# Two cross-attention layers on one core: first weights in parts, key-bias products moved, last batch projected with queries on partitions, a norm in two operations

## The chip, the cores and the metric

The kernel runs on one core of one Trainium2 chip. The metric is the time of one execution on the device, in microseconds. The kernel before took 739.87 us as the median of three runs (737.16 to 740.08). Its profiled execution took 736.62 us, of which the span from the first to the last instruction is 734.8 us.

## The reference, cut to what matters

Two layers of cross attention read the same context. There are 8 batches of 100 queries of width 1024, and 1444 context rows of width 512 per batch. All values are 32-bit floats.

```python
# layer 0: softmax over the 1444 keys, an output projection, a residual
Q = query @ Wq + bq;  K = key @ Wk + bk;  V = key @ Wv + bv
weights = softmax((Q @ K.T) / 32, axis=keys)
x = query + (weights @ V) @ Wo + bo

# layer 1: softmax over the 100 queries, a residual, a norm over the width of 1024
q = x @ Wq + bq;  k = latent @ Wk + bk;  v = latent @ Wv + bv
w = softmax((q @ k.T) / 32, axis=queries)
x = w @ v + x
return (x - mean(x)) * rsqrt(var(x) + 1e-6) * gamma + beta
```

The kernel never forms K and V. It multiplies weights with weights first (Wq Wk^T, and Wv Wo in layer 0), so that attention works on the context rows of width 512. Three consequences matter here. A bias of the keys gives one number per query, the sum over x and a vector Wq bk; the kernel calls it c0 in layer 0 and c1 in layer 1. In layer 1 the weights of a query don't sum to one, because the softmax runs over queries, so bv is multiplied by the sum of a query's weights (`r`). And in layer 1 the weighted context rows (`A1`, width 512) are multiplied by Wv (`wv1`) at the end.

## The kernel before: the parts that the change and its steps touch

The program order of TensorE is the order of the source. The orders of the other engines are decided when the program is built. Every matmul on 32-bit floats runs as two passes, so that a line with 64 products of the source shows 128 instructions.

```python
    psum = ctx.enter_context(tc.tile_pool(name="psum", bufs=8, ...))     # 8 banks
    ident = const.tile([P, P], ...);  make_identity(nc, ident)
    ones = const.tile([P, P], ...);   nc.vector.memset(ones, 1.0)

    def column(name, layout):              # six small bias columns
        nc.scalar.dma_start(out=t, in_=a[name].rearrange(layout, c=EC))

    def weight_products(name, left, right, l_width, r_width, scaled):
        for h in range(EC):                                     # 8 blocks of 128 rows
            st = unit(f"{name}_{h}")
            nc.sync.dma_start(out=st[:, :l_width], in_=lsrc[:, h, :])
            nc.sync.dma_start(out=st[:, l_width:], in_=rsrc[:, h, :])
            for ps, (i, j) in zip(banks, blocks):               # 8 products of 128x512
                nc.tensor.matmul(ps, st[:, i*P:(i+1)*P], st[:, l_width + j*512 : ...], ...)   # L111
            ...                                                 # VectorE: columns scaled and summed
```

The start of the program, with the key-bias products of layer 0 between the queries and the next weights:

```python
    wqk0, (acc_c, acc_u) = weight_products("qk0", ...)
    ...                                                         # xT loaded, u0, bqbk0, wqbk0
    for g in range(B // G):
        gT[0][g] = queries(0, g, wqk0, u0)                      # L175
    for g in range(B // G):                                     # two groups of four batches
        acc = key_bias_sums(f"kb0_{g}", g * GT, (g + 1) * GT, wqbk0)   # VectorE, L163/L165, one buffer "kb"
        for i in range(G):
            nc.tensor.matmul(ps[:T, b:b+1], acc[:, i*T:(i+1)*T], ones[:, 0:1], ...)   # L203
    nc.vector.tensor_scalar(c0, ps[:T, :B], SCALE, bqbk0[:T], ALU.mult, ALU.add)      # L204
    wvo, (acc_o,) = weight_products("vo0", ...)
    nc.vector.tensor_tensor(out_bias, out_bias, totals("bvo_ps", acc_o, EC), ALU.add) # L137, L208
    wqk1, (acc_c, acc_u) = weight_products("qk1", ...)
```

The end of the program, layer 1 from its weighted rows on:

```python
    def attend1(s, dst):
        ...                                # VectorE: part and wsum, the weights of a query summed
        weighted_rows(b, w, c, dst, ...)   # L256, then a VectorE copy from PSUM to dst (L264)
        nc.tensor.matmul(ps[:T, 0:1], wsum[:n], ones[:n, 0:1], ...)        # L382
        nc.vector.tensor_copy(s["r"], ps[:T, 0:1])

    def project1(b0, n, A):                # embedding on partitions, n*T queries as columns
        for e in range(EC):
            for k in range(LC):
                nc.tensor.matmul(ps[:, :n*T], wv1[:, k, e*P:(e+1)*P], A[:, k, :n*T], ...)   # L392
            nc.vector.tensor_tensor(to, to, ps[:, :n*T], ALU.add)                           # L396, to = xT[:, e, t0:t1]

    def finish(s):
        for j in range(2):
            for e in range(4):
                nc.tensor.transpose(ps[:T, ...], xT[:, 4*j+e, b*T:(b+1)*T], ident)          # L406
            nc.vector.scalar_tensor_tensor(z[:, half], bv1[:T, half], s["r"], ps[:T, :], ALU.mult, ALU.add)  # L408
            nc.vector.bn_stats(stats[:, j, :], z[:, half])                                  # L409
        nc.vector.bn_aggr(mv, ...)                                                          # L411
        nc.vector.tensor_scalar(rstd, mv[:, 1:2], EPS, None, ALU.add)                       # L413
        nc.gpsimd.tensor_tensor(rstd, rstd, mhalf[:T], ALU.pow)                             # L414
        nc.vector.tensor_scalar(z, z, mv[:, 0:1], rstd, ALU.subtract, ALU.mult)             # L415
        nc.gpsimd.tensor_tensor(z, z, gamma[:T], ALU.mult)                                  # L416
        nc.gpsimd.tensor_tensor(z, z, beta[:T], ALU.add)                                    # L417
        nc.gpsimd.dma_start(out=out[b], in_=z)                                              # L418

    for b in range(B):
        if b % 2 == 0:
            A1 = work.tile([P, LC, GT], ...)
        attend1(batches[b], A1[:, :, b % 2 * T : (b % 2 + 1) * T])
        if b == 0:
            ...                                            # queries and c1 of the second group
        if b + 2 < B:
            scores1(batches[b + 2], c1[(b + 2) // G])      # L343
        if b % 2:
            project1(b - 1, 2, A1)
            finish(batches[b - 1])
            finish(batches[b])
```

Of the kernel before, what the change touches and what calls it, by code (L numbers as in the profile page):

```python
# [30 lines left out]
P = 128  # L31
# [9 lines left out]
G = 4  # L41
# [6 lines left out]
def two_layer_cross_attention(ctx: ExitStack, tc: tile.TileContext, a: dict, out: bass.AP):  # L48
# [20 lines left out]
        return work.tile([P, S], F32, tag="prob", name=name, bufs=3)  # L69


    ident = const.tile([P, P], F32, tag="ident", name="ident")
    make_identity(nc, ident)
    ones = const.tile([P, P], F32, tag="ones", name="ones")
    nc.vector.memset(ones, 1.0)
    mhalf = const.tile([P, 1], F32, tag="mhalf", name="mhalf")
    nc.vector.memset(mhalf, -0.5)

    def column(name, layout):
        t = const.tile([P, EC], F32, tag=name, name=name)  # L80
        nc.scalar.dma_start(out=t, in_=a[name].rearrange(layout, c=EC))
        return t

    cols = {
# [6 lines left out]
    def weight_products(name, left, right, l_width, r_width, scaled):  # L91

        accs = []
        for v, side in scaled:
            if (l_width if side == 0 else r_width) == E:
                accs.append(row(f"{name}_{v}"))
            else:  # L100
                accs.append(work.tile([P, L], F32, tag="half", name=f"{name}_{v}", bufs=1))
        blocks = [(i, j) for i in range(l_width // P) for j in range(r_width // 512)]
        banks = [bank(f"{name}_{i}_{j}") for i, j in blocks]
        lsrc = a[left].rearrange("(p c) n -> p c n", c=EC)
        rsrc = a[right].rearrange("(p c) n -> p c n", c=EC)
        for h in range(EC):
            st = unit(f"{name}_{h}")
            nc.sync.dma_start(out=st[:, :l_width], in_=lsrc[:, h, :])
            nc.sync.dma_start(out=st[:, l_width:], in_=rsrc[:, h, :])
            for ps, (i, j) in zip(banks, blocks):  # L110
                nc.tensor.matmul(  # L111
                    ps,
                    st[:, i * P : (i + 1) * P],
                    st[:, l_width + j * 512 : l_width + (j + 1) * 512],
                    start=(h == 0),
                    stop=(h == EC - 1),
                )
            for acc, (v, side) in zip(accs, scaled):
                src = st[:, :l_width] if side == 0 else st[:, l_width:]
                if h == 0:  # L120
                    nc.vector.tensor_scalar(acc, src, cols[v][:, h : h + 1], None, ALU.mult)
                else:
                    nc.vector.scalar_tensor_tensor(acc, src, cols[v][:, h : h + 1], acc, ALU.mult, ALU.add)  # L123
        dst = weights.tile([P, l_width // P, r_width], F32, tag="w", name=name)
        for n, (ps, (i, j)) in enumerate(zip(banks, blocks)):
            to = dst[:, i, j * 512 : (j + 1) * 512]
            if n % 2:
                nc.scalar.copy(to, ps)
            else:
                nc.vector.tensor_copy(to, ps)  # L130
        return dst, accs
# [24 lines left out]

    def key_bias_sums(name, t0, t1, wqbk):

        acc = work.tile([P, GT], F32, tag="kb", name=name)
        for k in range(EC):  # L160
            src = xT[:, k, t0:t1]
            if k == 0:
                nc.vector.tensor_scalar(acc, src, wqbk[:, k : k + 1], None, ALU.mult)  # L163
            else:
                nc.vector.scalar_tensor_tensor(acc, src, wqbk[:, k : k + 1], acc, ALU.mult, ALU.add)  # L165
        return acc
# [27 lines left out]
    gT = [[None, None], [None, None]]  # L194
    for g in range(B // G):
        gT[0][g] = queries(0, g, wqk0, u0)
    c0 = const.tile([T, B], F32, tag="c0", name="c0")
    ps = bank("c0_ps")
    for g in range(B // G):
        acc = key_bias_sums(f"kb0_{g}", g * GT, (g + 1) * GT, wqbk0)  # L200
        for i in range(G):
            b = g * G + i
            nc.tensor.matmul(ps[:T, b : b + 1], acc[:, i * T : (i + 1) * T], ones[:, 0:1], start=True, stop=True)  # L203
    nc.vector.tensor_scalar(c0, ps[:T, :B], SCALE, bqbk0[:T], ALU.mult, ALU.add)  # L204


    wvo, (acc_o,) = weight_products("vo0", "L0_xattn_WvT", "L0_xattn_Wo", L, E, (("L0_xattn_bv", 1),))
    nc.vector.tensor_tensor(out_bias, out_bias, totals("bvo_ps", acc_o, EC), ALU.add)  # L208


    wqk1, (acc_c, acc_u) = weight_products(
# [38 lines left out]
    def weighted_rows(b, w, c, dst, name):  # L250

        ps = bank(name)
        for m in range(MC):
            r = held(m)
            for k in range(LC):
                nc.tensor.matmul(  # L256
                    ps[:, k * T : (k + 1) * T],
                    c[m // CQ][:r, m % CQ, k * P : (k + 1) * P],
                    w[:r, m, :],
                    start=(m == 0 and k == 0),  # L260
                    stop=(m == MC - 1),
                    skip_group_check=True,
                )
        nc.vector.tensor_copy(dst, ps[:, :GT].rearrange("p (c t) -> p c t", t=T))  # L264


    def scores0(s):
# [50 lines left out]
    def key_bias1(g):  # L318

        acc = key_bias_sums(f"kb1_{g}", g * GT, (g + 1) * GT, wqbk1)  # L320
        ps = bank(f"c1_ps{g}")
        nc.tensor.matmul(ps[:, :GT], ones, acc, start=True, stop=True)
        c1 = work.tile([P, GT], F32, tag="c1", name=f"c1_{g}", bufs=2)
        nc.vector.tensor_scalar(c1, ps[:, :GT], SCALE, bqbk1, ALU.mult, ALU.add)
        return c1

# [40 lines left out]
            )  # L367
        s["w"] = w

    def attend1(s, dst):  # L370
        b, w = s["b"], s["w"]
        c = load_rows(b)
        part = work.tile([P, GT], F32, tag="kb", name=f"part_{b}")[:, :T]
        wsum = work.tile([P, T], F32, tag="wsum", name=f"wsum_{b}", bufs=1)
        last = MC - 1
        nc.vector.tensor_copy(wsum[: held(last)], w[: held(last), last, :])
        nc.vector.tensor_reduce(part[:MR], w[:MR, :last, :].rearrange("p c t -> p t c"), AX.X, ALU.add)
        nc.vector.tensor_tensor(wsum[:MR], wsum[:MR], part[:MR], ALU.add)
        weighted_rows(b, w, c, dst, f"A1_{b}")
        ps = bank(f"wsum_ps_{b}")  # L380
        n = held(last)
        nc.tensor.matmul(ps[:T, 0:1], wsum[:n], ones[:n, 0:1], start=True, stop=True)  # L382
        s["r"] = small.tile([T, 1], F32, tag="r", name=f"r_{b}", bufs=3)
        nc.vector.tensor_copy(s["r"], ps[:T, 0:1])

    def project1(b0, n, A):

# [7 lines left out]
            to = xT[:, e, t0:t1]  # L395
            nc.vector.tensor_tensor(to, to, ps[:, : n * T], ALU.add)  # L396

    def finish(s):

        b = s["b"]  # L400
        z = row(f"z_{b}")[:T]
        stats = small.tile([T, 2, 6], F32, tag="stats", name=f"stats_{b}")
        for j in range(2):
            ps = bank(f"z_{b}_{j}")
            for e in range(4):
                nc.tensor.transpose(ps[:T, e * P : (e + 1) * P], xT[:, 4 * j + e, b * T : (b + 1) * T], ident)  # L406
            half = slice(j * 512, (j + 1) * 512)
            nc.vector.scalar_tensor_tensor(z[:, half], bv1[:T, half], s["r"], ps[:T, :], ALU.mult, ALU.add)  # L408
            nc.vector.bn_stats(stats[:, j, :], z[:, half])  # L409
        mv = small.tile([T, 2], F32, tag="mv", name=f"mv_{b}")  # L410
        nc.vector.bn_aggr(mv, stats.rearrange("p a n -> p (a n)"))  # L411
        rstd = small.tile([T, 1], F32, tag="rstd", name=f"rstd_{b}")
        nc.vector.tensor_scalar(rstd, mv[:, 1:2], EPS, None, ALU.add)  # L413
        nc.gpsimd.tensor_tensor(rstd, rstd, mhalf[:T], ALU.pow)  # L414
        nc.vector.tensor_scalar(z, z, mv[:, 0:1], rstd, ALU.subtract, ALU.mult)  # L415
        nc.gpsimd.tensor_tensor(z, z, gamma[:T], ALU.mult)  # L416
        nc.gpsimd.tensor_tensor(z, z, beta[:T], ALU.add)  # L417
        nc.gpsimd.dma_start(out=out[b], in_=z)  # L418


    batches = [{"b": b} for b in range(B)]
# [26 lines left out]

    scores1(batches[0], c1[0])
    weighted0(G + 3)  # L450
    bv1 = row_on_all("L1_xattn_bv")
    gamma = row_on_all("L1_xattn_gamma")
    beta = row_on_all("L1_xattn_beta")
# [1 line left out]
    project0(1, A0[1])  # L455
    wv1 = weights.tile([P, LC, E], F32, tag="w", name="wv1")
    nc.gpsimd.dma_start(out=wv1, in_=a["L1_xattn_Wv"].rearrange("(c p) e -> p c e", p=P))
    A1 = None
    for b in range(B):
        if b % 2 == 0:  # L460
            A1 = work.tile([P, LC, GT], F32, tag="AT", name=f"A1T_{b}", bufs=2)
        attend1(batches[b], A1[:, :, b % 2 * T : (b % 2 + 1) * T])
        if b == 0:
            gT[1][1] = queries(1, 1, wqk1, u1)
            c1[1] = key_bias1(1)
        if b + 2 < B:
            scores1(batches[b + 2], c1[(b + 2) // G])
        if b % 2:
            project1(b - 1, 2, A1)
            finish(batches[b - 1])  # L470
            finish(batches[b])


# [22 lines left out]
```

## Time and profile before

| what | value |
|---|---|
| time, median of 3 | 739.87 us |
| span of the profiled execution | 734.8 us |
| TensorE busy | 702.8 us, 96% |
| VectorE busy | 251.5 us, 34% |
| ScalarE busy | 78.0 us, 11% |
| GpSimd busy | 49.5 us, 7% |
| mean granted TensorE clock | 0.981 |
| moved by DMA | 124.73 MB, 170 GB/s over the span |

PE is TensorE's matmul, PEld its weight load, DVE VectorE, ACT ScalarE, POOL GpSimd, SP SyncE. A line number such as L203 is a line of the kernel. In the chain of work that ended last and in the timeline the first column is the start in us from the start of the span, the second the duration in us, and "x96" the number of instructions merged. In the list of waits the three numbers are the total in us, how many there were, and the longest in us. In a table by stretches of time the columns are the stretch, its length, the busy time of each engine with its instructions in brackets, the granted clock as a share of full speed, the share of the DMA engines, and GB/s.

### The profile page before, as it was taken

Reading aid. Unit: us, or ns where it says so; the run is one execution under the profiler, and the core shown is the slowest. Engines: PE = TensorE matmul, PEld = TensorE weight load, DVE = VectorE, ACT = ScalarE, POOL = GpSimd, SP = SyncE. Lnnn points to the kernel's source line nnn. Section 1 sums busy time; section 2 is a strip of 40 time slices with the busy share of each in tenths; the row PEclk is TensorE's granted clock in tenths of the full one; section 3 lists DMA queues with packets and bytes.
Section 4 is the critical chain, followed back from the end, with each engine's and each line's share of the span. In section 5 each row is a group of like instructions: output and inputs, shape, how many; then the busy total and the mean of one; then the engine's idle time right before and its main releaser. Section 6 shows DMA issues by size and latency. Waiting matters only on the chain.

```text
span 734.8 us, 8978 instructions
## 1 busy us (share of the span) xinstructions
PE 702.8 (96%) x3848; PEld 514.7 (70%) x3848; DVE 251.5 (34%) x404; ACT 78.0 (11%) x261; POOL 49.5 (7%) x42
## 2 busy tenths in 40 slices
PE   6999997999999999999999999999999999999980
PEld 3445553444445678885675889867799999999980
DVE  6346002321002412224300224440245745745633
ACT  0001010001001201110000113200112012012000
POOL 0000000000000000000000000000000600600606
PEclk9999998999999999999999999999999999999995
DMA  8952001333344999999052999958197798794101
GB/s 302 389 217 86 1 0 41 92 123 88 116 117 92 281 279 263 248 264 276 7 162 71 249 258 270 262 123 266 44 245 198 218 257 221 215 244 113 46 0 45
DMA packets 70696, 124.73 MB, mean 170 GB/s; under 512 B 4897, under 2 KB 39713, under 8 KB 70657
## 3 DMA queue, kind: packets, MB, share of 16 engines
q1 hardware_dynamic: 66912, 117.19, 57.9%
q0 software_dynamic: 1984, 6.95, 3.0%
q8 instruction: 30, 0.49, 0.3%
q10 hardware_dynamic: 1760, 0.02, 0.1%
q14 instruction: 10, 0.07, 0.0%
HBM read 120.87 MB, written 3.28 MB: 169 GB/s over the span
## 4 chain that ended last, share of the span: by engine, by line
PE 83%; issue 9%; POOL 4%; DVE 2%; DMA 1%; POOLq 0%; SPq 0%
PE A L256 18%; PE qk L111 15%; PE g L175 12%; PE s L278 11%; PE s L343 8%; PE vo L111 8%; PE o L311 6%; PE o L392 3%; POOL z L416 2%; POOL z L417 1%; PE pT L301 1%; DVE z L415 1%; DVE kb L165 1%; DMA qk<-in_L_xattn_WkT 1%; PE wqbk_ps L137 1%
## 5 line engine op out<-in xcount | busy, mean ns | idle before, releaser
L256 PE MATMUL A<-w,c 120*128 120x100 f32 (+1 forms) x1536 | 174.7, 275 | 0.0
L256 PEld LDWEIGHTS A<-w,c 120*128 120x128 f32 (+1 forms) x1536 | 172.8, 192 | 1.0
L111 PE MATMUL qk<-qk 128*128 128x512 f32 x256 | 112.7, 603 | 5.6 <-DMA qk<-in_L_xattn_WkT 5.6
L111 PEld LDWEIGHTS qk<-qk 128*128 128x128 f32 x256 | 49.4, 194 | 67.3 <-issue 61.5
L175 PE MATMUL g<-xT,qk 128*128 128x400 f32 x256 | 86.7, 500 | 0.0
L343 PE MATMUL s<-g1T,cT 128*120 128x100 f32 (+1 forms) x768 | 83.1, 270 | 0.0
L343 PEld LDWEIGHTS s<-g1T,cT 128*120 128x120 f32 (+1 forms) x768 | 82.2, 186 | 0.3 <-issue 0.2
L278 PE MATMUL s<-cT,g0T 128*100 128x360 f32 (+1 forms) x256 | 80.3, 473 | 0.0
L175 PEld LDWEIGHTS g<-xT,qk 128*128 128x128 f32 x256 | 48.4, 190 | 36.5
L278 PEld LDWEIGHTS s<-cT,g0T 128*100 128x100 f32 x256 | 43.0, 170 | 34.1 <-issue 1.7
L111 PE MATMUL vo<-vo 128*128 128x512 f32 x128 | 56.8, 607 | 0.0
L361 ACT ACTIVATE w<-w,negmax 120x100 f32<-120x100 f32 (+1 forms) x96 | 35.1, 367 | 147.4 <-DVE negmax L359 147.4
L111 PEld LDWEIGHTS vo<-vo 128*128 128x128 f32 x128 | 24.9, 196 | 31.2 <-issue 31.2
L281 DVE TENSOR_SCALAR p<-s,c 100x360 f32<-100x360 f32 (+1 forms) x32 | 19.0, 594 | 78.6 <-PE s L278 78.5
L392 PE MATMUL o<-A1T,wv 128*128 128x200 f32 x256 | 44.1, 333 | 0.6 <-DVE A1T L264 0.6
L392 PEld LDWEIGHTS o<-A1T,wv 128*128 128x128 f32 x256 | 43.2, 190 | 0.7 <-DVE A1T L264 0.7
L311 PE MATMUL o<-A0T,vo 128*128 128x400 f32 x128 | 43.3, 499 | 0.0
L311 PEld LDWEIGHTS o<-A0T,vo 128*128 128x128 f32 x128 | 24.2, 190 | 18.3
L123 DVE SCALAR_TENSOR_TENSOR qk_L_xattn_bk<-qk,L_xattn_bk,qk_L_xattn_bk 128x1024 f32<-128x1024 f32 x14 | 18.0, 1284 | 33.6 <-DMA qk<-in_L_xattn_WqT 33.6
L446 POOL DMA_DIRECT2D L_xattn_bv<-in_L_xattn_bv x1 | 0.7, 696 | 405.5 <-PE pT L301 405.5
L130 DVE COPY qk<-qk 128x512 f32<-128x512 f32 x8 | 5.5, 691 | 56.3 <-PE qk L111 56.3
L264 DVE COPY A0T<-A 128x400 f32<-128x400 f32 x8 | 4.6, 574 | 57.0 <-PE A L256 57.0
(77 smaller groups left out, 385.5 us busy)
## 6 DMA issues: line engine op xcount, KB each, us to landing
cT<-in_ctxT SPq DMA_DIRECT2D x64, 728.0 KB
c<-in_ctx SPq DMA_DIRECT2D x64, 720.0 KB
qk<-in_L_xattn_WqT SPq DMA_DIRECT2D x16, 512.0 KB
qk<-in_L_xattn_WkT SPq DMA_DIRECT2D x16, 256.0 KB
vo<-in_L_xattn_Wo SPq DMA_DIRECT2D x8, 512.0 KB
xT<-in_xT SPq DMA_DIRECT2D x2, 1600.0 KB
out<-z POOLq DMA_DIRECT2D x8, 400.0 KB, 3.7
vo<-in_L_xattn_WvT SPq DMA_DIRECT2D x8, 256.0 KB
```

The costliest lines, as they stand in the source:

```text
L111: nc.tensor.matmul(ps, st[:, i * P : (i + 1) * P], st[:, l_width + j * 512 : l_width + (j + 1) * 512], start=(h == 0), stop=(h == EC - 1),)
L123: nc.vector.scalar_tensor_tensor(acc, src, cols[v][:, h : h + 1], acc, ALU.mult, ALU.add)
L137: nc.tensor.matmul(ps[:, c : c + 1], acc[:, c * P : (c + 1) * P], ones[:, 0:1], start=True, stop=True)
L175: nc.tensor.matmul(ps[:, :GT], w[:, k, c * P : (c + 1) * P], xT[:, k, t0:t1], start=(k == 0), stop=(k == EC - 1))
L256: nc.tensor.matmul(ps[:, k * T : (k + 1) * T], c[m // CQ][:r, m % CQ, k * P : (k + 1) * P], w[:r, m, :], start=(m == 0 and k == 0), stop=( ...
L278: nc.tensor.matmul(ps[:T, :n], q0[:, k, t0 : t0 + T], cT[q][:, k, :n], start=(k == 0), stop=(k == LC - 1))
L281: nc.vector.tensor_scalar(p[:, q * QR : q * QR + n], ps[:T, :n], SCALE, c0[:, b : b + 1], ALU.mult, ALU.add)
L311: nc.tensor.matmul(ps[:, :GT], wvo[:, k, e * P : (e + 1) * P], A[:, k, :], start=(k == 0), stop=(k == LC - 1))
L343: nc.tensor.matmul(ps[:r, (m - m0) * T : (m - m0 + 1) * T], cT[m // CQ][:, k, o : o + r], q1[:, k, t0 : t0 + T], start=(k == 0), stop=(k = ...
L361: nc.scalar.activation(w[:r, m, :], w[:r, m, :], AF.Exp, bias=negmax[:r, m : m + 1], accum_out=total[:r, m : m + 1])
L392: nc.tensor.matmul(ps[:, : n * T], wv1[:, k, e * P : (e + 1) * P], A[:, k, : n * T], start=(k == 0), stop=(k == LC - 1))
L416: nc.gpsimd.tensor_tensor(z, z, gamma[:T], ALU.mult)
```

## The change

It does these things.

- Eight products of `ones` with `ones` stand at the head of TensorE's program, ahead of any data. `ones` is made first.
- The first block of weights comes in three transfers instead of two: the right operand and half of the left one from SyncE, the other half of the left one from ScalarE. The six bias columns are loaded from GpSimd's queue.
- The key-bias products of layer 0 (L203) move behind the products of `wvo`. Both groups' sums have a buffer of their own.
- The sum of a batch's weights with its product (`wsum`, `r`) becomes a function of its own, called one batch earlier.
- Layer 1 is projected in groups of 3, 2, 2 and 1 batches instead of 2, 2, 2, 2. The group of one, the last batch, is transposed before its attention (`untransposed`), and its projection puts queries on partitions and 512 columns of the embedding in one product (`project_last`), so that the result needs no transpose.
- The norm's end becomes two VectorE operations, (z - mean) * gamma and then z * rstd + beta, in the place of one on VectorE and two on GpSimd. For the last batch the second is done in halves, each with its own transfer, from SyncE and ScalarE.
- The last batch's copy of `A1` from PSUM is ScalarE's.

```diff
+    ones = const.tile([P, P], F32, tag="ones", name="ones")
+    nc.vector.memset(ones, 1.0)
+    warm = bank("warm")
+    for _ in range(8):
+        nc.tensor.matmul(warm[:, :P], ones, ones, start=True, stop=True)
...
-        nc.scalar.dma_start(out=t, in_=a[name].rearrange(layout, c=EC))
+        nc.gpsimd.dma_start(out=t, in_=a[name].rearrange(layout, c=EC))
...
-            nc.sync.dma_start(out=st[:, :l_width], in_=lsrc[:, h, :])
-            nc.sync.dma_start(out=st[:, l_width:], in_=rsrc[:, h, :])
+            if h == 0 and name == "qk0":
+                nc.sync.dma_start(out=st[:, l_width:], in_=rsrc[:, h, :])
+                nc.scalar.dma_start(out=st[:, : l_width // 2], in_=lsrc[:, h, : l_width // 2])
+                nc.sync.dma_start(out=st[:, l_width // 2 : l_width], in_=lsrc[:, h, l_width // 2 :])
+            else:
+                ...                                        # the two lines as before
...
-        acc = work.tile([P, GT], F32, tag="kb", name=name)
+        acc = work.tile([P, GT], F32, tag="kb", name=name, bufs=3)
...
+    kb0 = [key_bias_sums(f"kb0_{g}", g * GT, (g + 1) * GT, wqbk0) for g in range(B // G)]
+    wvo, (acc_o,) = weight_products("vo0", ...)
+    nc.vector.tensor_tensor(out_bias, out_bias, totals("bvo_ps", acc_o, EC), ALU.add)
     c0 = const.tile([T, B], F32, tag="c0", name="c0")
     ps = bank("c0_ps")
-    for g in range(B // G):
-        acc = key_bias_sums(f"kb0_{g}", g * GT, (g + 1) * GT, wqbk0)
-        for i in range(G):
-            ...
+    for b in range(B):
+        t0 = b % G * T
+        nc.tensor.matmul(ps[:T, b : b + 1], kb0[b // G][:, t0 : t0 + T], ones[:, 0:1], start=True, stop=True)
     nc.vector.tensor_scalar(c0, ps[:T, :B], SCALE, bqbk0[:T], ALU.mult, ALU.add)
-    wvo, (acc_o,) = weight_products("vo0", ...)
-    nc.vector.tensor_tensor(out_bias, out_bias, totals("bvo_ps", acc_o, EC), ALU.add)
...
-        nc.vector.tensor_copy(dst, ps[:, :GT].rearrange("p (c t) -> p c t", t=T))
+        src = ps[:, :GT].rearrange("p (c t) -> p c t", t=T)
+        if name == f"A1_{B - 1}":
+            nc.scalar.copy(dst, src)
+        else:
+            nc.vector.tensor_copy(dst, src)
...
-        nc.vector.tensor_scalar(z, z, mv[:, 0:1], rstd, ALU.subtract, ALU.mult)
-        nc.gpsimd.tensor_tensor(z, z, gamma[:T], ALU.mult)
-        nc.gpsimd.tensor_tensor(z, z, beta[:T], ALU.add)
-        nc.gpsimd.dma_start(out=out[b], in_=z)
+        nc.vector.scalar_tensor_tensor(z, z, mv[:, 0:1], gamma[:T], ALU.subtract, ALU.mult)
+        parts = 2 if b == B - 1 else 1
+        for j in range(parts):
+            w = slice(j * E // parts, (j + 1) * E // parts)
+            nc.vector.scalar_tensor_tensor(z[:, w], z[:, w], rstd, beta[:T, w], ALU.mult, ALU.add)
+            (nc.scalar if j else nc.gpsimd if parts == 1 else nc.sync).dma_start(out=out[b][:, w], in_=z[:, w])
...
+    def project_last(s, A):
+        for j in range(2):
+            ps = bank(f"ol_{j}")
+            half = slice(j * 512, (j + 1) * 512)
+            for k in range(LC):
+                nc.tensor.matmul(ps[:T, :], A[:, k, :T], wv1[:, k, half], start=(k == 0), stop=(k == LC - 1))
+            nc.vector.tensor_tensor(s["z"][:, half], s["z"][:, half], ps[:T, :], ALU.add)
+            statistics(s, j)
+        normalise(s)
...
-    for b in range(B):
-        ...                                                # as shown above
+    for b0, n in ((0, 3), (3, 2), (5, 2), (7, 1)):
+        A1 = work.tile([P, LC, GT], F32, tag="AT", name=f"A1T_{b0}", bufs=2)
+        if b0 == B - 1:
+            untransposed(batches[b0])                      # transposes, z = bv1 * r + x
+        for b in range(b0, b0 + n):
+            attend1(batches[b], A1[:, :, (b - b0) * T : (b - b0 + 1) * T])
+            if b == 0:
+                ...                                        # queries and c1 of the second group
+            if b + 2 < B:
+                scores1(batches[b + 2], c1[(b + 2) // G])
+            if b + 1 < B:
+                weight_sums(batches[b + 1])
+        if b0 == B - 1:
+            project_last(batches[b0], A1)
+        else:
+            project1(b0, n, A1)
+            for b in range(b0, b0 + n):
+                finish(batches[b])
```

## The prediction

> **What bounds the kernel now.** I read the page's slices first, then the chain of waits in order of time, then the list of waits, then tables by stretches around the places that stood out.
>
> ```profile
> PE   6999997999999999999999999999999999999980
> POOL 0000000000000000000000000000000600600606
> ```
>
> TensorE is busy in every slice but the first, one near 110 us, and the last two. So the kernel is bound by TensorE, and only four things can move its time: when TensorE starts, the hole near 110 us, how much work TensorE has, and what follows its last product. POOL is the other way round: it works only where batches are finished, and in the last slice, where TensorE is done.
>
> The chain of waits shows head and hole:
>
> ```profile
> 5.63 57.52 PE qk L111 x128
> ...
> 109.05 0.64 PE c_ps L203 x8
> ...
> 114.89 1.49 PE c_ps L203 x8
> 116.38 56.71 PE vo L111 x128
> 173.08 1.68 PE bvo_ps L137 x16
> 174.76 55.04 PE qk L111 x128
> ```
>
> The same 128 instructions take 57.52, 56.71 and 55.04 us, so the first lost 2.5 us and the second 1.7 us against the third. Between 109.05 and 116.38 us the program did 16 tiny products, 7.3 us in all. The waits say for whom:
>
> ```profile
> PE qk L111 <- DMA qk<-in_L_xattn_WkT: 5.6, 1, 5.6
> PE c_ps L203 <- DVE kb L165: 5.2, 1, 5.2
> PE o L392 <- DVE A1T L264: 0.6, 1, 0.6
> ```
>
> The 5.2 us are VectorE's eight sums of the second group, which can't begin before the first group's products have freed the one buffer. Why the products behind the hole are slow, a table of TensorE by stretches shows (its clock stands behind the busy time):
>
> ```profile
> 114.00:116.00 2.00, 1.11 (x7) 0.50 0.00 0
> 116.00:118.00 2.00, 2.00 (x5) 0.50 0.00 0
> 118.00:120.00 2.00, 2.00 (x4) 0.60 0.00 0
> 120.00:122.00 2.00, 2.00 (x6) 1.00 0.00 0
> ```
>
> The clock falls to a half in the hole and returns 4.7 us after work resumes. The end, from the timeline and a last stretch with all engines:
>
> ```profile
> 701.43 11.09 PE L392 MATMUL o<-A1T,wv 128*128 128x200 f32 x64 [0.57 <-DVE A1T L264]
> 712.36 1.91 PE L406 MATMUL z<-ident,xT 128*100 128x128 f32 x16
> 718.61 2.34 POOL L416 TENSOR_TENSOR z<-z,L_xattn_gamma 100x1024 f32<-100x1024 f32 x1 [0.93 <-DVE z L415]
> 721.43 2.33 POOL L417 TENSOR_TENSOR z<-z,L_xattn_beta 100x1024 f32<-100x1024 f32 x1
> 721.49 2.82 DVE L415 TENSOR_SCALAR z<-z,mv,rstd 100x1024 f32<-100x1024 f32 x1 [1.93 <-POOL rstd L414]
> 724.39 2.34 POOL L416 TENSOR_TENSOR z<-z,L_xattn_gamma 100x1024 f32<-100x1024 f32 x1 [0.63 <-DVE z L415]
> 727.32 2.35 POOL L417 TENSOR_TENSOR z<-z,L_xattn_beta 100x1024 f32<-100x1024 f32 x1
> 729.96 0.56 POOL L418 DMA_DIRECT2D out<-z x1 [0.29 <-POOL z L417]
> 714.30:734.80 20.50, 0.00 (x0) 0.00 (x0) 7.94 (x13) 0.00 (x0) 11.52 (x8) 0.56 0.13 40
> ```
>
> TensorE is done at 714.3 us and the span ends at 734.8: 20.5 us of tail, in which two batches queue for POOL.
>
> [...] weight loads of L111 start 0.85 us apart up to 10.5 us and 0.43 us apart after, so it took 4.9 us from the first product to full speed, and 4.7 us behind the hole. (The granted clock reads 1.00 in the first stretch all the same; I trust the spacing.) [...] L415 takes 0.81 us alone and 2.82 us beside L417. [...] L123, the same operation on 128x1024, takes 1.28 us, while L415 on one tensor takes 0.81. [...] The trace has 0.41 us per issue here, so I credit the second queue with little, and the smaller first transfer with most.
>
> **The change, part by part.**
>
> *Head.* The first weights are 512 + 256 KB, issued at 0.75 and 1.21 us, both landed by 5.6. The first four products now need 256 + 256 KB. At the 391 GB/s that the stretch from 10 to 20 us shows, 256 KB less are 0.65 us: start near 4.9 instead of 5.63, -0.7. The ones-products can start when `ones` is filled, near 1.1 us (the memset took 0.17). 16 passes of 128 columns, at 0.855 us for 512 columns when cold, are 0.21 us each, 3.4 us: they end near 4.5, before the data. If full speed again comes 4.8 us after the first product, it comes at 5.9, plus some doubt for the small pause[...]; I take 6.5. Then 1.6 us of real products are cold and lose half of it, 0.8, instead of 2.4: -1.6. Head: -2.3.
>
> *The hole.* With both sums on VectorE beside the queries (8 x 0.65 us each against 43 us of L175), the wait is gone. The 7.33 us become 16 products at some 0.09 us, 1.5 us: -5.8. The clock stays up in front of `vo`: -1.7. But the products now follow the 16 of `bvo_ps`, together 3.2 us of one-column work. The 2.8 us of such work near 230 us let the clock fall in one of two places in this trace (0.50 from 233 to 235 us, not after 66 us); that cost 1.55 us in L278 (20.97 for 64 instructions against 2 x 9.71). Half a chance of it, +0.8. The hole: -6.7.
>
> *TensorE's own work in layer 1.* L392 takes 10.85 us for 64 passes of 200 columns, four times: 43.4. L311 takes 21.49 for 64 of 400, so a column costs 0.84 ns in both. The group of three is 64 x 300 columns, 16.2 us; two groups of two are 21.7; the last is 16 passes of 512 columns at 0.43, 6.9. Sum 44.8: +1.4. Transposes are as many as before. The wait for the copy of A1 (0.6 us, before the last projection, where no scores stand between) now comes twice, before the group of batches 5 and 6 and before the last: +0.7.
>
> *Tail.* Ahead of it only batch 7 is left. After the last product: the add from PSUM 0.73 (as L408), statistics 0.68, aggregate 0.20, epsilon 0.15, then (z - mean) * gamma at 1.28, beside which POOL does its power in 0.57; the first half of the last operation 0.73, the second 0.73: 4.5 us. The issue of the second half then stands where that of 729.96 stood, and from there to the end were 4.85 us for 400 KB by POOL's queue. For 200 KB by ScalarE's I estimate 3.7, since the shortest landing of the old rows is 3.2 and 200 KB are 0.5 us at 391 GB/s less. Tail: 8.2 instead of 20.5, -12.3. The work of batches 5 and 6 after their transposes is some 13 us of VectorE (six halves at 0.73, four statistics at 0.68, four operations at 1.28), beside attention of 10.7 us plus 3.5 for the first half of the projection: just hidden.
>
> *Sum.* -2.3 - 6.7 + 1.4 + 0.7 - 12.3 = -19.2, from 739.87: 720.7, rounded to 720.5.
>
> **The rivals.** (a) VectorE becomes the wait. Three batches finish together after the first group: six halves at 0.73, six statistics at 0.68, six operations at 1.28 and small ones, 17 us against 10.7 of attention and 3.4 of scores before the next eviction. In the order as built, the next copy of A1 and the score evictions stand among them, not behind all; VectorE is at 43 to 57% there[...]. If it fails, TensorE waits 2 to 4 us once or twice: 723 to 727. (b) The tail is hidden less: if the last batch waits for VectorE's work of batches 5 and 6, the 12.3 become some 9: 724. (c) The clock eats the head: if the ones-products, which lie before an idle pause, don't count, the head gives 0.7 only, and if the joined one-column products do drop the clock, 0.8 more is lost: 723. (d) DMA: attention and scores need 2.9 MB per 10.5 us, and five now run without a projection between. Eight ran so in layer 0 (254 to 340 us) with TensorE never waiting, so I give this little.
>
> **Range and chances.** The parts that are removed waits (5.8) and the tail (12) are sure in kind; the uncertain ones are the clock (3 us either way; the runs of the kernel before differ by 2.9) and VectorE's order. So 715.5 to 725.5. Faster by 2% means under 725.1: 0.87. Within 2%: 0.12. Slower would need a new wait of over 30 us, which no buffer here suggests: 0.01.
>
> **What would show it.** Right: first L111 product near 4.9 us and its 128 passes in some 55.9 us; no wait of TensorE for L165's sums; `vo` in 55.0; projections at 16.2, 10.85, 10.85 and 6.9 us; at most 8.5 us after the last product; no POOL work on z. Wrong: TensorE waiting for VectorE between 550 and 700 us, a late start of the weights, or a half clock in the products of qk after the joined one-column products; most wrong, a tail over 12 us.

## The result and the profile after

The changed kernel takes 718.97 us as the median of four runs (718.8 to 721.73), the kernel before 738.51 beside it (736.88 to 740.08). The ratio is 0.9744, with a 95% interval of 0.9708 to 0.9781. The profiled execution has a span of 716.8 us in the place of 734.8. (The line numbers moved: L119 is now the weight products, L183 the queries, L214 the key-bias products, L405 the projection, L453 the last batch's projection, L434 and L438 the norm's two operations.)

The page's slices, TensorE and GpSimd:

```profile
PE   9999999999999999999999999999999999999994
POOL 2000000000000000000000000000000003002011
```

The gap near 110 us and the empty last slice are gone; behind its first slice, GpSimd only starts transfers and computes a power per batch. The waits of TensorE for another engine or for data that are left, apart from the one ahead of the ones-products (1.1 us for `ones`; the profile names the fill next to it, `mhalf`):

```profile
PE ol L453 <- ACT A1T L273: 0.6, 1, 0.6
PE o L405 <- DVE A1T L275: 0.6, 1, 0.6
PE qk L119 <- DMA qk<-in_L_xattn_WkT: 0.3, 1, 0.3
```

The chain in order of time (start, duration, what):

```profile
5.11 55.72 PE qk L119 x128
...
63.62 44.79 PE g L183 x128
108.40 54.93 PE vo L119 x128
163.34 1.68 PE bvo_ps L145 x16
165.01 1.41 PE c_ps L214 x16
166.43 56.74 PE qk L119 x128
...
225.96 19.50 PE s L289 x64
...
569.95 16.27 PE o L405 x64
...
630.90 10.94 PE o L405 x64
...
676.03 11.09 PE o L405 x64
...
701.02 7.12 PE ol L453 x16
```

Set beside the chain of before: the first 128 passes fell from 57.52 to 55.72 us, the key-bias products from 7.33 to 1.41, the products of `vo` from 56.71 to 54.93. But the queries rose from 43.09 to 44.79, and the next weights from 55.04 to 56.74, with the same instructions. The first scores (`s`) fell from 20.97 to 19.50. The end, from the timeline:

```profile
709.93 1.27 DVE L434 SCALAR_TENSOR_TENSOR z<-z,mv,L_xattn_gamma 100x1024 f32<-100x1024 f32 x1
710.17 1.46 POOL L433 TENSOR_TENSOR rstd<-rstd,mhalf 100x1 f32<-100x1 f32 x1 [9.69 <-DVE rstd L432]
711.66 1.42 DVE L438 SCALAR_TENSOR_TENSOR z<-z,rstd,L_xattn_beta 100x512 f32<-100x512 f32 x2 [0.46 <-POOL rstd L433]
713.11 0.57 ACTq L439 DMA_DIRECT2D out<-z x1
```

TensorE's last pass ends at 708.15 us (701.02 + 7.12), so the tail is 8.65 us in the place of 20.5.

### The profile page after: what moved, and what is told of

Same layout as the page of the kernel before. It is cut to its first block, busy times and chain, and to the rows that moved or that the text cites. A ratio compares the mean times of both kernels' runs of the same rounds, so it can differ in the third digit from the quotient of the medians.

```text
span 716.8 us, 8925 instructions
## 1 busy us (share of the span) xinstructions
PE 705.7 (98%) x3816; PEld 509.8 (71%) x3816; DVE 242.5 (34%) x406; ACT 78.5 (11%) x262; POOL 22.8 (3%) x31
## 4 chain that ended last, share of the span: by engine, by line
PE 98%; DMA 1%; DVE 0%; POOLq 0%; DVEq 0%; issue 0%; ACT 0%
PE A L263 24%; PE qk L119 16%; PE g L183 12%; PE s L354 11%; PE s L289 11%; PE vo L119 8%; PE o L322 6%; PE o L405 5%; PE pT L312 1%; PE ol L453 1%; PE z L418 1%; DMA qk<-in_L_xattn_WkT 1%; PE wqbk_ps L145 0%; PE bvo_ps L145 0%; PE u_ps L145 0%; POOLq L536 0%
## 5 line engine op out<-in xcount | busy, mean ns | idle before, releaser
L119 PE MATMUL qk<-qk 128*128 128x512 f32 x256 | 112.6, 602 | 0.3 <-DMA qk<-in_L_xattn_WkT 0.3
L119 PEld LDWEIGHTS qk<-qk 128*128 128x128 f32 x256 | 49.3, 194 | 62.2 <-issue 61.7
L183 PE MATMUL g<-xT,qk 128*128 128x400 f32 x256 | 88.3, 507 | 0.0
L183 PEld LDWEIGHTS g<-xT,qk 128*128 128x128 f32 x256 | 49.2, 193 | 37.4 <-issue 1.6
L119 PE MATMUL vo<-vo 128*128 128x512 f32 x128 | 55.1, 592 | 0.0
L119 PEld LDWEIGHTS vo<-vo 128*128 128x128 f32 x128 | 24.3, 190 | 30.4 <-issue 30.1
L405 PE MATMUL o<-A1T,wv 128*128 128x200 f32 (+1 forms) x192 | 38.6, 362 | 0.6 <-DVE A1T L275 0.6
L405 PEld LDWEIGHTS o<-A1T,wv 128*128 128x128 f32 x192 | 33.7, 190 | 4.5 <-DVE A1T L275 0.7
L362 DVE SCALAR_TENSOR_TENSOR w<-s,c 120x400 f32<-120x400 f32 (+1 forms) x24 | 13.8, 575 | 36.9 <-PE s L354 36.9
```

The lines of the kernel that those rows point to most:

```text
L119: nc.tensor.matmul(ps, st[:, i * P : (i + 1) * P], st[:, l_width + j * 512 : l_width + (j + 1) * 512], start=(h == 0), stop=(h == EC - 1),)
L183: nc.tensor.matmul(ps[:, :GT], w[:, k, c * P : (c + 1) * P], xT[:, k, t0:t1], start=(k == 0), stop=(k == EC - 1))
L362: nc.vector.scalar_tensor_tensor(w[:r, grp, :], ps[:r, :GT].rearrange("p (c t) -> p c t", t=T), SCALE, c1[:r, t0 : t0 + T].unsqueeze(1).to ...
L405: nc.tensor.matmul(ps[:, : n * T], wv1[:, k, e * P : (e + 1) * P], A[:, k, : n * T], start=(k == 0), stop=(k == LC - 1))
```

## The experiments

My theory was that four things carry the change: an earlier, warmer start, the buffers that take the wait of 5.2 us away, a shorter tail, and a clock that falls after runs of one-column products and so gives and takes 1.5 to 1.8 us per fall. A fall is a stretch in which the granted clock drops to about a half of full speed (0.50 to 0.66 over 2 us in the changed kernel's profile). The rivals are named with each run. The runs belong to three sets on three chips. The kernel before took 737.24 us beside the set of the ones-products, the two first transfers, the old place and the pairs; 737.14 beside the buffers, the norm with GpSimd and the two widths; 737.5 beside the last four. Each kernel has one profiled execution.

### Without the ones-products

```diff
-    warm = bank("warm")
-    for _ in range(8):
-        nc.tensor.matmul(warm[:, :P], ones, ones, start=True, stop=True)
```

> The changed kernel without the eight ones-products at its head. Theory: they bring the clock up before the data are there. Without them the first 128 passes of L119 take some 57.5 us instead of 55.7, with weight loads 0.85 us apart up to about 10 us, and the time is about 720.8 us (1.8 more). Rival: the head gained from the smaller first transfer alone; then the first passes stay near 55.7 us and the time near 719.

Measured: 718.97 us (718.62 to 726.12), as the changed kernel. The profiled execution, which was the one at 726.12, has 58.06 us for the first 128 passes, but also 44.48 for the queries, 57.75 for the next weights and 22.43 for the first scores: the clock fell at three other places too. The other three have a mean granted clock of 0.995, three of the changed kernel's four 0.992, so fewer falls may have hidden a slower head. The median can't tell: falls elsewhere are as large as the effect. It was repeated below without the falls.

### Two first transfers

```diff
-            if h == 0 and name == "qk0":
-                ...                              # three transfers
-            else:
+            # for every block:
                 nc.sync.dma_start(out=st[:, :l_width], in_=lsrc[:, h, :])
                 nc.sync.dma_start(out=st[:, l_width:], in_=rsrc[:, h, :])
```

> The changed kernel with its first block of weights in two transfers from SyncE, as before the change. Theory: the first product waits for 256 KB more, starts near 5.6 us instead of 5.1, and the time grows by 0.5 us to some 719.5. Rival 1: the transfers end together anyhow: no difference. Rival 2: the longer pause between the ones-products (done at 4.8 us) and the data lets the clock stay down, and 1.8 us more are lost: 721.3.

Measured: 719.2 us (718.66 to 719.78); the first product starts at 5.37 us instead of 5.11, and the first passes take 55.26. So the parts bring the start forward by 0.3 us, half of what I expected, and rival 2 fails: behind the longer pause the first passes are no slower (55.26 us, 55.72 in the change). The first 128 passes end at 60.63 us here and at 60.82 in the change, so that a gain in time from the parts is not shown. The kernels here with three transfers started at 5.09 to 5.31 us, the two others with two transfers at 5.63 (before) and 5.27 (the buffers alone): about 0.25 us, and not always.

### The key-bias products in their old place

```diff
     kb0 = [key_bias_sums(f"kb0_{g}", g * GT, (g + 1) * GT, wqbk0) for g in range(B // G)]
+    c0 = ...; the 16 passes of L214 and c0's scaling, unchanged
     wvo, (acc_o,) = weight_products("vo0", ...)
     nc.vector.tensor_tensor(out_bias, out_bias, totals("bvo_ps", acc_o, EC), ALU.add)
-    c0 = ...
```

> The changed kernel with the 16 passes of the key-bias products back in their old place, straight after the queries, but with the buffers of the change. Theory: the wait of 5.2 us came from the one buffer, not from the place; no wait comes back. The one-column products then stand as 1.4 us at 108 us and 1.7 us at 163 us instead of 3.1 us together, so that the clock no longer falls behind them and the passes of the next weights take 55.0 us instead of 56.7: about 717.3. Rival: the place counts, VectorE's sums are late there, and TensorE waits again: 723 to 725.

Measured: 718.94 us (716.71 to 719.95). No wait came back: the 16 passes take 1.33 us there. The move isn't needed for the wait. The expected gain of 1.7 us in the median did not come. From the chain of its profiled execution (716.71, span 714.8):

```profile
164.35 55.04 PE qk L119 x128
...
222.18 21.19 PE s L289 x64
```

The next weights are at their short time, but the first scores take 21.19 us instead of 19.50: one fall, at another place. The other profiles say the same. In all five with the 32 passes joined (the change and the runs of the ones-products, the two transfers, the pairs and the norm with GpSimd), the next weights take 56.6 to 57.8 us; in the three with them apart (before, this one and the buffers alone), 55.04. The first scores are at 19.50 in four of the five, and at 20.85 to 21.19 in the three. So joining them brought a fall each time, and mostly spared the one that comes later.

### The buffers alone, in the kernel before

```diff
-        acc = work.tile([P, GT], F32, tag="kb", name=name)
+        acc = work.tile([P, GT], F32, tag="kb", name=name, bufs=3)
...
-        c1 = work.tile([P, GT], F32, tag="c1", name=f"c1_{g}", bufs=2)
+        c1 = work.tile([P, GT], F32, tag="kb", name=f"c1_{g}", bufs=3)
...                                              # part as well: tag "kb", bufs=3
```

> The kernel before with nothing changed but the buffers: the sums kb, part and c1 share three buffers instead of one and two. Theory: this alone removes the wait of 5.2 us: 7.3 us between the queries and the next weights become 1.4, so that the time falls from 737.2 to about 731.5, by up to 1.7 more where the clock does not fall there. Rival: the products must move as well; then no more than 1 us is won.

Measured: 728.47 us (727.59 to 732.45), ratio to before 0.9872 (0.9831 to 0.9913), 8.7 us less. The change shares these three buffers in the same way. From the chain:

```profile
5.27 56.57 PE qk L111 x128
...
107.73 1.33 PE c_ps L203 x16
109.05 55.04 PE vo L111 x128
```

7.33 us have become 1.33, and the products of `vo` no longer start cold (55.04 in the place of 56.71): 7.7 us from a buffer count. The rest is the head, which this kernel doesn't change: the first product starts 0.36 us earlier and its 128 passes take 0.95 us less, as executions differ.

### All in pairs

```diff
-    for b0, n in ((0, 3), (3, 2), (5, 2), (7, 1)):
+    for b0, n in ((0, 2), (2, 2), (4, 2), (6, 2)):
...                                              # no untransposed, no project_last
```

> The changed kernel with the projection in four groups of two, the last batch like the others, and the norm in two operations. Theory: TensorE's own work falls by 2.0 us and one wait of 0.6, but two batches stand behind the last product: some 12 us of VectorE and a transfer of 3.7, a tail of 14 to 15 us instead of 8.7; together 3 to 4 us more, 722 to 723. Rival: the order of the batches does nearly all of the tail, and the norm little: a tail near 20 us and 728.

Measured: 720.33 us (719.37 to 726.16). That is below the 722 to 723 expected, but the sum is disturbed by the falls again; it was repeated below. From the timeline of the profiled execution:

```profile
701.89 1.91 PE L418 MATMUL z<-ident,xT 128*100 128x128 f32 x16
```

TensorE's last pass ends at 703.8 us in a span of 717.4: a tail of 13.6 us, between the 8.65 of the change and the 20.5 of before. So of the 11.9 us by which the tail fell, the last batch's own form gave 5.0, part of which is paid back on TensorE. What this kernel keeps of the change gave 6.9: the norm's two operations, the sums moved, and the last result sent in halves from two queues. This run doesn't part these.

### The norm with GpSimd

```diff
-        nc.vector.scalar_tensor_tensor(z, z, mv[:, 0:1], gamma[:T], ALU.subtract, ALU.mult)
+        nc.vector.tensor_scalar(z, z, mv[:, 0:1], rstd, ALU.subtract, ALU.mult)
+        nc.gpsimd.tensor_tensor(z, z, gamma[:T], ALU.mult)
...
-            nc.vector.scalar_tensor_tensor(z[:, w], z[:, w], rstd, beta[:T, w], ALU.mult, ALU.add)
+            nc.gpsimd.tensor_tensor(z[:, w], z[:, w], beta[:T, w], ALU.add)
```

> The changed kernel, last batch alone and all, with the norm's old operations: one of VectorE, two of GpSimd. Theory: GpSimd's operations stand on the path behind the last product: 0.57 power, 0.81, 2.35, then two halves at 1.2, against the 1.8, 0.73 and 0.73 of the change: 3 us more, and up to 3 more if batches 5 and 6 still hold GpSimd: 722 to 725. Rival: with one batch alone at the end the norm's form hardly matters: 719 to 720.

Measured: 722.27 us (721.88 to 725.31), 3.3 more than the change: as the theory had it, at its lower edge. From its timeline:

```profile
709.91 0.56 POOL L433 TENSOR_TENSOR rstd<-rstd,mhalf 100x1 f32<-100x1 f32 x1 [3.97 <-DVE rstd L432]
711.40 2.34 POOL L435 TENSOR_TENSOR z<-z,L_xattn_gamma 100x1024 f32<-100x1024 f32 x1 [0.93 <-DVE z L434]
```

GpSimd had waited 3.97 us, so batches 5 and 6 were done. TensorE's last pass ends at 707.94 us in a span of 720.4, a tail of 12.5 us instead of 8.65: the norm's own operations are the whole difference. The power takes 0.56 us here and 1.46 in the change.

### One-column products made 64 columns wide

```diff
+W = 64
-            nc.tensor.matmul(ps[:, c : c + 1], acc[:, c * P : (c + 1) * P], ones[:, 0:1], start=True, stop=True)
-        return ps[:, :n]
+            nc.tensor.matmul(ps[:, c * W : (c + 1) * W], acc[:, c * P : (c + 1) * P], ones[:, 0:W], start=True, stop=True)
+        return ps.rearrange("p (n w) -> p n w", w=W)[:, :n, 0]
...                                              # c0 in the same way
```

> The changed kernel with the one-column products (the sums of a column, and c0) made 64 columns wide; only one of the 64 equal columns is read. Theory: the clock falls behind these products[...]; 64 columns fit beside the load, cost nothing[...], so that the falls behind 63, 166 and 226 us go: up to 3.4 us less than 718.97, about 715.6, and less spread between runs. Rival: 64 columns are [...]too few to count, or the falls have another cause: 719, with falls as before.

Measured: 715.15 us (714.94 to 715.61), ratio to before 0.9683 (0.9647 to 0.972); its slowest run is 3.2 us under the fastest of the changed kernel. From its chain:

```profile
63.26 43.04 PE g L186 x128
...
162.97 1.41 PE c_ps L217 x16
164.38 54.99 PE qk L120 x128
...
222.22 19.45 PE s L294 x64
```

Every group is at its short time at once, and the wide passes cost nothing: c0's 16 take 1.41 us in both, and where the others take 0.05 us more, the group behind them takes 0.05 less. TensorE by stretches, first of the changed kernel, then of this one (the clock stands behind the busy time):

```profile
64.00:66.00 2.00, 2.00 (x5) 0.56 0.19 73
168.00:170.00 2.00, 2.00 (x4) 0.50 0.00 0
```

```profile
64.00:66.00 2.00, 2.00 (x7) 1.00 0.02 7
166.00:168.00 2.00, 2.00 (x6) 1.00 0.00 0
```

The two falls of the change's profile (behind 63 and 166 us) are gone, by width alone. One profile could be luck, so here are all fourteen, by how many of the places had a fall in the passes or right behind them:

| run of passes without a gap | its length with no fall in it, us | places with a fall |
|---|---|---|
| one column: `bvo_ps` or `c_ps` alone | 1.3 to 1.7 | 0 of 5 |
| one column: `u_ps`, `bb_ps`, `wqbk_ps` (near 62 and 225 us) | 2.8 | 8 of 16 |
| one column: `bvo_ps` and `c_ps` joined | 3.1 | 5 of 5 |
| 64 or 128 columns: the second and third rows' places | 2.8 to 3.5 | 0 of 18 |

(The hole of the kernel before is left out. A fall is counted where the group behind the passes takes at least 1.3 us more than its short time; the others are within 0.1 us of it.) That width removes the falls is shown. Why is not: the profile counts narrow passes as busy like wide ones (2.00 of 2.00 us).

### 128 columns, overwritten

```diff
-            nc.tensor.matmul(ps[:, c : c + 1], ..., ones[:, 0:1], ...)
+            nc.tensor.matmul(ps[:, c : c + P], ..., ones, ...)
```

> As the one before, but 128 columns wide, each product overwriting all but one of the columns of the one before it. Theory: [...]as in the transposes, behind which no fall was seen; the falls go and the time is about 715.6, at no more than 0.2 us of extra passes. [...] Rival: 719 with falls as before.

Measured: 715.6 us (715.5 to 715.84), without falls. This width is not quite free: c0's 16 passes take 1.75 us in the place of 1.41. 64 columns are enough already; how few would do was not narrowed down further.

### Without the ones-products, free of falls

```diff
...                                              # W = 64 as above
-    warm = bank("warm")
-    for _ in range(8):
-        nc.tensor.matmul(warm[:, :P], ones, ones, start=True, stop=True)
```

> The kernel with 64-column products, without the eight ones-products at the head. With the other falls of the clock gone this shows the head alone. Theory: the first 128 passes of L119 take about 57.3 us instead of 55.2: 2 us more than 715.15, about 717.2. Rival, after the equal medians with and without them before: the ones-products bring nothing: 715.2.

Measured: 717.45 us (717.26 to 717.85), 2.3 more than with them. Its chain begins with

```profile
5.18 57.48 PE qk L117 x128
```

against 55.17 us in the 64-column kernel: the whole difference. The ones-products bring 2.3 us in this pair, which the first try had hidden. The head differs between executions: these passes took 55.17 to 56.18 us in the ten profiles with ones-products and 56.57 to 58.06 in the four without.

### In pairs, free of falls

```diff
...                                              # W = 64 as above
-    for b0, n in ((0, 3), (3, 2), (5, 2), (7, 1)):
+    for b0, n in ((0, 2), (2, 2), (4, 2), (6, 2)):
...                                              # no untransposed, no project_last
```

> The kernel with 64-column products and the projection in four pairs, norm in two operations. Shows the gain of the last batch alone, free of the clock. Theory: the tail grows by 5.0 us and TensorE saves 2.0 and one wait of 0.6: 2.3 us more than 715.15, about 717.5. Rival: within 0.5 of 715.15, the last batch's form being paid back by TensorE's own work.

Measured: 718.65 us (717.88 to 718.76), 3.5 more than 715.15. The span of its profiled execution, 715.9, is 2.9 us longer than the other's 713.0: TensorE's last pass ends 2.0 us earlier (702.3 for 704.3) and the tail is 4.9 us longer (13.6 for 8.7). The last batch's own form brings some 3 us. The theory had 2.3: it counted a wait of 0.6 us beside the 2.0, but the 2.0 hold it.

### The wait for A1 filled

```diff
...                                              # W = 64 as above
-        if b0 == B - 1:
-            untransposed(batches[b0])
...
         else:
+            if b0 + n == B - 1:
+                untransposed(batches[B - 1])
             project1(b0, n, A1)
```

> The kernel with 64-column products, and the transposes of the last batch moved ahead of the projection of batches 5 and 6. Theory: those eight passes (0.9 us) fill TensorE's wait of 0.6 us for the copy of A1, so that the time falls from 715.15 to about 714.5. Rival: VectorE then has the last batch's two halves (1.5 us) ahead of the sums of the projection, which stand in the way of its banks: 715 to 716.

Measured: 714.99 us (714.36 to 715.1). A gain of 0.2 us against the ranges of both isn't shown. The profiles tell more. From the chains, first of the 64-column kernel, then of this one, the first and the last group of passes:

```profile
5.24 55.17 PE qk L120 x128
...
697.22 7.12 PE ol L458 x16
```

```profile
5.14 56.18 PE qk L120 x128
...
697.34 7.12 PE ol L458 x16
```

The wait of L410 is gone from TensorE's list, and from the end of the first 128 passes to the last TensorE needs 643.1 us in the place of 643.9. The gain of the theory is there, 0.8 us, but the first 128 passes took 1.0 us more in this execution and hid it. VectorE's two halves, the rival, cost TensorE no wait.

### Groups of 4, 3 and 1

```diff
...                                              # W = 64 and untransposed moved, as above
-        s["r"] = small.tile([T, 1], F32, tag="r", name=f"r_{b}", bufs=3)
+        s["r"] = small.tile([T, 1], F32, tag="r", name=f"r_{b}", bufs=6)
...
-    for b0, n in ((0, 3), (3, 2), (5, 2), (7, 1)):
+    for b0, n in ((0, 4), (4, 3), (7, 1)):
```

> As the first of these, with groups of 4, 3 and 1 batches in the place of 3, 2, 2 and 1 (six buffers for r). Theory: 64 passes of 400 columns (21.5 us) and 64 of 300 (16.3) replace 16.3, 10.9 and 11.1: 0.5 us less, about 714.0. Rival: four batches finish together, some 22 us of VectorE, and the evictions of the next scores, which stand behind them, come late: TensorE waits some 5 us, 719.

Measured: 714.43 us (714.04 to 714.62), ratio to before 0.9672 (0.9647 to 0.9698), the lowest of all, 0.6 us under the kernel with groups of 3, 2, 2 and 1 and the wait filled. From its chain:

```profile
5.27 55.60 PE qk L120 x128
...
696.84 7.12 PE ol L458 x16
```

Again the head decides: from the end of the first 128 passes to its last, TensorE needs 643.1 us here as there. So the 0.6 us can't be credited to the groups; the ranges of both overlap, too. VectorE's work on the four batches caused no wait of TensorE, where the rival had some 5 us; the rival fails. The kernel is 4.5 us under the changed one, 3.8 of which the 64 columns gave.

## Why the prediction was right

The prediction said 720.5 us and the change brought 718.97. Part of this nearness is luck. The steps were read from an execution of 736.62 us, but taken off a median of 739.87. Taken off 736.62 they give 717.4, and the profiled execution after took 718.8: the steps promised 1.4 us too much, and the starting point, 3.2 us higher, more than made up for it. The steps, by the two profiles:

| step | predicted, us | measured, us |
|---|---|---|
| start of the first product | -0.7 | -0.5 (5.63 to 5.11) |
| first 128 passes warmer | -1.6 | -1.8 (57.52 to 55.72) |
| the wait at the key-bias products | -5.8 | -5.9 (7.33 to 1.41) |
| clock: `vo` | -1.7 | -1.8 |
| clock: behind the joined one-column products | +0.8 | +1.7 |
| clock: elsewhere (queries +1.7, first scores -1.5) | 0 | +0.2 |
| TensorE's work in projections | +1.4 | +1.8 (43.6 to 45.4) |
| waits for A1 | +0.7 | +0.6 |
| tail | -12.3 | -11.9 (20.5 to 8.65) |
| sum | -19.2 | -17.6, and the spans differ by 18.0 |

*The head* was right in sum and in cause: the experiment without falls shows 2.3 us for the ones-products. The share given to the smaller first transfer was too large: where the parts were undone, the start came 0.3 us later, not 0.7. That the second queue brings little was its estimate, from 0.41 us per issue; no run parts the queue from the smaller transfer. The 6.5 us at which it put full speed, 0.6 behind the 5.9 of its own sum, were an estimate as well; in the change's trace the weight loads are 0.43 us apart from 6.6 us on.

*The hole* was right in its wait. The text spoke of both sums "beside the queries" and credited the change; the runs show that the buffers alone do it, and the move of the products does nothing for the wait.

*The clock* was the mis-sized term. "Half a chance of it" was taken for one place. In fact the joined passes brought a fall in all five profiles that have them, the half clock in the products of `qk` that the prediction lists as a sign of being wrong. The runs of 2.8 us brought one in 8 of 16 places, the queries of the change among them. So the change paid 3.4 us for two falls (the queries and the next weights) in its profile, which ate what the warm `vo` and the warm first scores had given (3.2). The three clock rows of the table come to +0.1 in the place of -0.9.

*TensorE's work* was 0.4 short: the groups took 16.27, 10.94, 11.09 and 7.12 us, not 16.2, 10.85, 10.85 and 6.9 (and those before 43.6 in all, not 43.4). *The tail* was 0.4 longer: the power took 1.46 us beside L434, not the 0.57 it was given, so the last operation began 0.5 us late. The 1.28 us for the new form were L123's, on two tensors of 128x1024; L434 took 1.27. The 3.7 us given to the last transfer came true (713.11 us to the end at 716.8), but they don't follow from the numbers beside them: 3.2 less 0.5 is 2.7, and 4.85 less 0.5 is 4.35.

*The rivals.* (a) and (d) failed: TensorE has no wait for VectorE other than for A1, none for data after the start, even with four batches together. (b) didn't come: VectorE was idle for 5.1 us before the first half of the last projection was there. (c) held in its second part (the joined products dropped the clock), and failed in its first.

## What to carry to other kernels

Count the copies that a reduction needs before moving its consumer: a second buffer gave here what a reordering seemed to give (7.33 to 1.33 us). Where TensorE bounds a kernel, don't leave it with runs of one-column products (2.8 us of them brought falls here): widen them as far as it costs nothing, here to 64 columns, which took 3.8 us off the time and brought the spread of the runs from 2.9 to 0.7 us. Compare variants of a few us only once the falls are gone (the same 2.8 us of passes brought one at 8 of 16 places), or read the groups' times in the profile rather than the medians.

## What the runs showed of the hardware

The clock falls though TensorE's instructions leave no gap in the trace (0.56 and 0.50 in stretches with 2.00 us busy of 2.00): 2.8 us of one-column passes, 0.1 us apart, were enough at 8 of 16 places and 3.1 us at 5 of 5, while 1.7 us or less never were (5 places). With 64 columns a pass or 128 there was no fall at any of the 18 places in the profiles of six kernels.

GpSimd's power on 100x1 elements takes 0.56 us with VectorE at rest (the norm with GpSimd) and 1.46 beside L434, which reads two tensors, z and gamma: it ends 0.43 us after L434 does (711.63 and 711.20). In the change this comes once per batch (1.46 to 1.54 us in all eight, 0.54 to 0.57 in the kernel before), and for the last one it is on the path: VectorE waits 0.46 us for it.
